# Two layers of graph and expert blocks: 12 instead of 8 of 16 node groups routed, in parts of 5 and 7, with the first part's pairs beside the second part's lists

## The chip, the cores and the metric

The kernel runs on one core of one Trainium2 chip. The time is device microseconds of one execution, given as the median of several runs. Its engines are PE (matrix multiply), DVE (vector), ACT (activation), POOL (which here mostly issues indirect DMAs) and SP (which issues the plain DMAs). They run side by side and meet at semaphores. "PEld" is the loading of weights into PE.

## The reference

The input is x, 128 graphs of 64 nodes with 256 features (8192 nodes), and an adjacency array. Two layers follow, each a graph block and an expert block, with residuals. The change concerns the last block alone, the expert block of layer 1:

```python
h = (x_flat @ W_gat).reshape(M, HEADS, NUM_EXPERTS)            # 4 heads, 4 experts
e = leaky_relu(a_src[src] + a_dst[dst])                         # 1,048,576 edges and loops
alpha = exp(e - e_max[dst]) / denom[dst]
agg = segment_sum(h[src] * alpha[:, :, None], dst)              # per node
scores = _layernorm(agg, ln_gamma, ln_beta).reshape(M, HEADS, NUM_EXPERTS).mean(1)
topk_s, topk_i = top_k(scores, 2)
w = softmax(topk_s)
for ei in range(NUM_EXPERTS):
    g = where(topk_i == ei, w, 0).sum(-1)
    hh = gelu(x @ W1[ei] + b1[ei])                              # 256 -> 512
    out = out + g[..., None] * (hh @ W2[ei] + b2[ei])           # 512 -> 256
```

Each node needs two of four experts, but which two is known only when the sums over its edges are there.

## The kernel before

The 8192 nodes are 64 tiles of 128, in 16 groups (`NG`) of four tiles (`GR`). All of x stays in SBUF. Layer 0 takes about the first 1000 us and is not touched. Layer 1 has these stages, with the times of the profiled execution:

**Graph stage** (1000 to 1381 us). A loop over steps `s` moves the groups through five streams (`back`, `first`, `second`, `combine`, `tables`), each some steps behind the other. `tables(g)` writes the normalised group to HBM: transposed to `zts` for a dense group, plain to `zns` for a routed one. It also writes the node table `tsrc` that the edges read.

**Dense groups.** A group of the first `DENSE` = 8 is put through all four experts without waiting for the gates. The generator `units` (lines 1129 to 1148) yields after every piece of that work: an expert has eight units, four of "h" (256 to 512, line 1101, with a gelu on ACT) and four of "y" (512 to 256, line 1111, with a bias add on DVE, line 1115). There are 256 units. As long as the gates aren't known, the y's are stored in `ystore` (128 KB each) and added later by `kept()`; once `adds` is filled, they are added at once, times the gate. Units need only the weights and `zts`, so they can stand beside anything. The graph stage takes 56 of them: from step 12 on, `quota` says how many follow each round of the streams.

**Prologue** (1381 to 1425 us): 20 units beside the set-up of the edge work.

**Lists** (1425 to 1706 us). The edges were sorted earlier into 16 lists, one for each group of destination nodes; `lists` has those of the routed groups first. `edges_of_lists` has 9 steps (`ET`) a list, 162 in all with the tail of its pipeline. Every step has an indirect gather of 128 rows of `tsrc` by POOL (line 1578, tile `got`) and a small copy, and by its place in the list the steps also sort a later list (lines 1507 to 1556), find the destinations' values (`to`, `pd`, `one`, `fd`), make the messages and one-hot matrices (`ol`, `r`) and sum them by matmul (line 1623) into `acc`. Three of four steps are followed by a unit. Every third step clears 256 KB of `zslots`.

**Gates, route, send.** When a part's lists are in `acc`, `gates` (27 yields, nearly all DVE) makes its two weights a node, and `route` (8 yields) finds for each node the two rows that it gets in the experts' slots (`place`) and which expert each slot belongs to (`pair_e`). `send` loads each tile of `zns` back, copies it twice into `y` tiles and scatters them to `zslots[h]` with two indirect DMAs by POOL (line 1897). The 8 routed groups are two parts of four groups, 16 tiles, 32 sends each. The first part's sends end beside units, at 1742 us; while they go, the dense groups' gates are made.

**Pairs** (1742 to 2028 us). A pair is two tiles of slots of one expert. A part has `PAIRS` = 19 (16 and three for experts that end within a pair). `load` (line 2014) reads the pair's expert into registers, then SP issues `zin` (256 KB), `w1e` (512 KB), `b1e` and `b2e`, two pairs ahead; `turned` transposes `zin`; h and y follow (lines 2059 and 2072), and y goes to `yslots[h]`. A pair has seven yields. Beside the first part's pairs stand the second part's sends, one at every third yield; beside the second part's pairs stands `back(0)`.

**Return and tail** (2028 to 2101 us). `back(h)` gathers a tile's two results from `yslots[h]` by POOL (line 2093), copies them, and adds them with their weights (line 2104) to x, which is then stored. `back(1)` needs all of the second part's y's, and stands beside the last 40 units.

The order on each engine comes from the framework: program order gives priorities, and it may issue an instruction earlier where its inputs and buffers are there. `paced_copy` and `tc.issue_after` put an instruction behind a given one on its engine. A pool's `bufs` says how many buffers each tile name has.

## Time and profile before

| | |
|---|---|
| median of 17 runs | 2104.31 us (2098.69 to 2109.7) |
| the profiled execution's own time | 2102.73 us |
| its span | 2101.0 us |
| busy: PE / PEld / DVE / ACT / POOL | 91% / 65% / 64% / 45% / 23% |
| PE: dense units, lines 1101 and 1111 | 512 and 1024 matmul records |
| PE: pairs, lines 2059 and 2072 | 139.2 and 137.8 us, 608 records each |
| POOL: gathers of line 1578 | 144, mean 1067 ns |
| POOL: sends of line 1897, returns of line 2093 | 64 each, mean 978 and 1002 ns |

The profile gives busy times by engine and by group of instructions, waits with what ended them, the chain of work that ended last, and sums over stretches of time. Busy PE time has modelled ends, and a matmul in 32 bit shows as two records. An engine's idle time costs something only where the chain passes through it.

### The profile page before, as it was taken

The page shows a single profiled execution, that of the slowest core. Times are in us where ns is not written, and L with a number is a line of the kernel's source. Part 1 is how long each engine was busy: PE and PEld are TensorE (multiplying, and loading weights), DVE is VectorE, ACT ScalarE, POOL GpSimd, SP SyncE. Part 2 cuts the span into 40 slices and gives each one's busy share as a digit, 9 for nine tenths or more (in the row PEclk, how much of TensorE's full clock was granted, in tenths as well). Part 3 has the DMA queues.
Part 4 walks back from the last instruction along what each step waited for, and adds up shares of the span by engine and source line. Part 5 has one row for each costly group of instructions (what it writes and reads, how often), then busy time and mean ns, then how long its engine had stood idle before and what let it go on. Part 6 is the DMA issues. An engine that isn't in the chain of part 4 may idle for free. (4 is left out here: it accounts for less than half of the span.)

```text
span 2101.0 us, 32601 instructions
## 1 busy us (share of the span) xinstructions
PE 1915.8 (91%) x10566; PEld 1371.3 (65%) x10566; DVE 1338.3 (64%) x4351; ACT 939.4 (45%) x1719; POOL 493.6 (23%) x528
## 2 busy tenths in 40 slices
PE   7889989899976999999578899998999999999999
PEld 5444545454435899898346667766667767888876
DVE  6889888842115888886697755756688451333435
ACT  4867766767641222221365565432333333333432
POOL 2013122132230000000530100004566552303223
PEclk9999999999997999999787899999999999999999
DMA  8022223233227555544214101282223248978943
GB/s 241 27 93 103 90 86 110 80 132 126 102 102 222 163 159 152 161 153 133 83 52 147 52 32 62 97 236 70 53 64 64 49 152 250 296 256 271 285 128 98
DMA packets 229376, 274.96 MB, mean 131 GB/s; under 512 B 57936, under 2 KB 173520, under 8 KB 229200
## 3 DMA queue, kind: packets, MB, share of 16 engines
q1 hardware_dynamic: 194288, 212.26, 32.6%
q0 software_dynamic: 24064, 60.22, 9.1%
q8 instruction: 89, 1.46, 0.3%
q10 hardware_dynamic: 10848, 0.30, 0.3%
q14 instruction: 87, 0.71, 0.1%
HBM read 159.40 MB, written 113.22 MB: 130 GB/s over the span
## 5 line engine op out<-in xcount | busy, mean ns | idle before, releaser
L464 PE MATMUL ph<-zT,w 128*128 128x512 f32 x512 | 249.0, 611 | 5.2 <-ACT zT L700 3.8
L969 PE MATMUL py<-wd,hTt 128*128 x1088 | 247.2, 381 | 0.0
L969 PEld LDWEIGHTS py<-wd,hTt 128*128 128x128 f32 x1088 | 202.5, 191 | 25.0
L954 ACT COPY hTt<-th 128x512 f32<-128x512 f32 x136 | 73.2, 589 | 299.7 <-PE th L951 299.7
L773 POOL DMA_INDIRECT hrows<-rows,pos x128 | 128.0, 1000 | 306.7 <-issue 189.0
L1578 POOL DMA_INDIRECT got<-tsrc,esrc x144 | 153.6, 1067 | 193.6 <-DMA ystore<-y 84.5
L1111 PE MATMUL py<-w,hT 128*128 128x256 f32 x800 | 190.5, 389 | 8.1 <-DVE td L1939 4.2
L1101 PE MATMUL ph<-zT,w 128*128 128x512 f32 x400 | 183.2, 599 | 0.0
L1180 POOL DMA_INDIRECT yin<-yrows,row_y x64 | 63.1, 987 | 485.8 <-SPq L1024 370.1
L1111 PEld LDWEIGHTS py<-w,hT 128*128 128x128 f32 x800 | 150.4, 193 | 38.6 <-issue 10.8
L464 PEld LDWEIGHTS ph<-zT,w 128*128 128x128 f32 x512 | 94.0, 195 | 106.5 <-issue 87.8
L1105 ACT ACTIVATE hT<-ph,b 128x512 f32<-128x512 f32 x100 | 68.6, 688 | 196.1 <-PE ph L1101 173.5
L2063 ACT ACTIVATE hT<-ph,b1e 128x256 f32<-128x256 f32 x152 | 72.1, 474 | 177.1 <-PE ph L2059 104.0
L2059 PE MATMUL ph<-zTp,w1e 128*128 128x256 f32 x608 | 139.2, 382 | 3.7 <-DMA w1e<-in_L_ffn_W_dram 3.7
L2072 PE MATMUL py<-w,hT 128*128 x608 | 137.8, 379 | 0.9 <-issue 0.9
L2080 DVE TENSOR_TENSOR y<-py,b2e 128x256 f32<-128x256 f32 x76 | 32.3, 425 | 156.0 <-PE py L2072 144.5
L2059 PEld LDWEIGHTS ph<-zTp,w1e 128*128 128x128 f32 x608 | 116.6, 192 | 20.2 <-issue 4.0
L626 PE MATMUL pre<-wd 128*128 128x512 f32 x256 | 124.2, 602 | 1.9 <-ACT wd L612 1.3
L467 ACT ACTIVATE hT<-ph,b 128x512 f32<-128x512 f32 x128 | 88.0, 687 | 77.3 <-PE ph L464 59.6
L2072 PEld LDWEIGHTS py<-w,hT 128*128 128x128 f32 x608 | 112.6, 190 | 15.1 <-issue 1.3
L1101 PEld LDWEIGHTS ph<-zT,w 128*128 128x128 f32 x400 | 73.0, 190 | 70.9 <-issue 69.8
L201 DVE TENSOR_TENSOR one<-iota_l,pb 128x2048 bf16<-128x2048 bf16 x96 | 116.8, 1217 | 0.2
(413 smaller groups left out, 3737.0 us busy)
## 6 DMA issues: line engine op xcount, KB each, us to landing
hin<-hrows SPq DMA_DIRECT2D x136, 256.0 KB
w1e<-in_L_ffn_W_dram SPq DMA_DIRECT2D x38, 512.0 KB
yin<-ystore SPq DMA_DIRECT2D x24, 512.0 KB
ystore<-y SPq DMA_DIRECT2D x80, 128.0 KB
zslots<-none SPq DMA_DIRECT2D x38, 256.0 KB
zin<-zslots SPq DMA_DIRECT2D x38, 256.0 KB
yslots<-y SPq DMA_DIRECT2D x76, 128.0 KB
bd<-in_L_ffn_bd_dram SPq DMA_DIRECT2D x68, 128.0 KB
```

What stands on the lines that cost most here:

```text
L201: V.tensor_tensor(o, numbers.unsqueeze(1).to_broadcast(shape), of.rearrange("p (j e) -> p j e", e=2).unsqueeze(2).to_broadcast(shape), ALU ...
L464: nc.tensor.matmul(ph, w1[:, c, q * P : q * P + P], zT[:, c, :], start=(c == 0), stop=(c == 1))
L467: gelus.append(S.activation(hT, ph, AF.Gelu, bias=b1[:, q : q + 1]).ins)
L626: nc.tensor.matmul(pre, xnT[:, c, n * P : n * P + P], wcat[:, c, :], start=(c == 0), stop=(c == 1),)
L773: nc.gpsimd.indirect_dma_start(to, bass.IndirectOffsetOnAxis(ap=pos[:, t : t + 1], axis=0), of[:, k, :], None)
L954: S.copy(hT[:, i : i + GR, :].rearrange("p q n -> p (q n)"), th)
L969: nc.tensor.matmul(py, hT[:, q, :], wd[:, bass.ds(e, 1), q, :].rearrange("p e f -> p (e f)"), start=(q == 0), stop=(q == NH - 1),)
L1101: nc.tensor.matmul(ph, w1[:, e, c, q * P : q * P + P], zT[:, c, :], start=(c == 0), stop=(c == 1))
L1111: nc.tensor.matmul(py, hTs[q][:, k * P : k * P + P], w2[:, e, q, :], start=(q == 0), stop=(q == NH1 - 1))
L1578: nc.gpsimd.indirect_dma_start(got, None, tsrc, bass.IndirectOffsetOnAxis(ap=esrc[:, b, at : at + 1], axis=0))
L2059: nc.tensor.matmul(ph, w1e[:, c, q * P : q * P + P], zT[:, c, :], start=(c == 0), stop=(c == 1))
L2072: nc.tensor.matmul(py, hTs[q][:, k * P : k * P + P], w2[:, e, q, :].rearrange("p e f -> p (e f)"), start=(q == 0), stop=(q == NH1 - 1),)
```

## The change

The first 5 and then 7 groups after the dense ones are routed, so that 4 groups are dense (128 units) and 12 routed (20 and 28 tiles; 23 and 31 pairs; 40 and 56 sends and as many returns). In the graph stage one unit follows the third round of each step from step 12 on. The pools of the lists, gates, sends and pairs are all open together; to that end most of the lists' tiles become single, the pools of hT and y tiles get 6 and 4 buffers instead of 8 and 6, `zin` two and `zTp` one instead of three, `kept` loads one expert's 128 KB at a time, `back` gathers into the space of `ts` and `td` and adds from there without a copy, and `td3` lies in that of `on`. `gates` works in place in `acc`.

The order is written anew: 55 list steps with a unit at every other; the first part's routing, three yields to each step and unit; its sends, two to a unit; eight more units behind the first loads of the pairs. Then come the pairs. Beside the first part's stand five list steps to six yields, up to the end of the second part's lists, then its routing, two yields at a time, then its sends, one at a yield. Beside the second part's pairs stand the remaining steps (those of the dense groups' lists), the dense groups' gates, then `kept`, and `back(0)` at every third yield. The last 24 units stand beside `back(1)`, two yields to a unit. A slot pair is cleared at every step until all 54 are.

```diff
-PARTS = 2
-ROUTED = 4 * PARTS
-DENSE = NG - ROUTED
-RT = ROUTED // PARTS * GR
-PAIRS = RT + 3
+ROUTED = (5, 7)
+PARTS = len(ROUTED)
+DENSE = NG - sum(ROUTED)
+RT = [GR * n for n in ROUTED]
+T0 = [GR * (DENSE + sum(ROUTED[:h])) for h in range(PARTS)]
+PAIRS = [n + NEXP - 1 for n in RT]
...
-                at = s - TABLES - 2
-                if s >= NG + SECOND:
-                    quota = int(r < 3)
-                elif at >= 0:
-                    quota = (2 * (at % 2), 2 * (at % 2), 4 - 4 * (at % 2), 0, 0, 0, 0, 0)[r]
-                else:
-                    quota = 0
+                quota = int(s >= TABLES + 2 and r == 2)
...
-    def edges_of_lists(pool, psum, td3):
+    def edges_of_lists(pool, one_each, psum, td3):
...
-                    el = pool.tile([P, ET * P], BF16, name="el")
+                    el = one_each.tile([P, ET * P], BF16, name="el")
...
-    hp = ctx.enter_context(tc.tile_pool(name="hp", bufs=8, reuse_waits="tile"))
-    yp = ctx.enter_context(tc.tile_pool(name="yp", bufs=6, reuse_waits="tile"))
+    hp = ctx.enter_context(tc.tile_pool(name="hp", bufs=6, reuse_waits="tile"))
+    yp = ctx.enter_context(tc.tile_pool(name="yp", bufs=4, reuse_waits="tile"))
...
             for j in range(2):
                 z = to["y"]()
                 paced_copy(z, zn)
-                sent = nc.gpsimd.indirect_dma_start(
+                row = nc.gpsimd.indirect_dma_start(
                     zslots[h], bass.IndirectOffsetOnAxis(ap=place[h][:, j, t : t + 1], axis=0), z, None
                 )
                 for other in sends:
-                    tc.declare_no_dep(sent.ins, other, reason="no two write the same row")
-                sends.append(sent.ins)
+                    tc.declare_no_dep(row.ins, other, reason="no two write the same row")
+                sends.append(row.ins)
                 yield
...
-        steps = routes()
-        zeros = ((h, i) for h in range(PARTS) for i in range(PAIRS))
-        for taken, _ in enumerate(edges_of_lists(emp, psm, td3)):
-
-            if taken % 3 == 0:
-                for h, i in zeros:
-                    nc.sync.dma_start(
-                        zslots[h][2 * P * i : 2 * P * i + 2 * P].rearrange("(k p) f -> p k f", p=P),
-                        none.unsqueeze(1).to_broadcast([P, 2, D]),
...
-            if taken > ET * (ROUTED // PARTS + 2):
-                next(steps, None)
-
-            if taken >= ET * NB:
-                next(sending)
-            if taken % 4 != 3:
-                next(units)
-        for _ in steps:
-            pass
+        sent.append(h)
...
+    KEEP = 1
...
-        ts = [t for t in range(T0) if n_kept[t // GR]]
-        for n in range(len(ts) + 1):
-            if n < len(ts):
-                g, k = divmod(ts[n], GR)
-                ys[n] = f2.tile([P, NEXP * D], F32, name="yin")[:, 0 : n_kept[g] * D]
+        of = [
+            (t, e, min(KEEP, n_kept[t // GR] - e))
+            for t in range(T0[0])
+            for e in range(0, n_kept[t // GR], KEEP)
+        ]
+        for n in range(len(of) + 1):
+            if n < len(of):
+                t, e, m = of[n]
+                g, k = divmod(t, GR)
+                ys[n] = f2.tile([P, KEEP * D], F32, name="yin")[:, 0 : m * D]
                 with tc.issue_after(behind[0]):
-                    nc.sync.dma_start(ys[n], ystore[g, k, :, 0 : n_kept[g] * D])
+                    nc.sync.dma_start(ys[n], ystore[g, k, :, e * D : (e + m) * D])
...
-    with tc.tile_pool(name="gd", bufs=1, reuse_waits="tile") as gd:
-        steps = gates(gd, 0, T0, {})
-        for _ in sending:
-            next(steps, None)
-            next(steps, None)
-            g, n = next(units)
-        for _ in steps:
-            pass
-        while (n + 1) % (NH1 + GR):
-            g, n = next(units)
-    adds.append(add)
...
-            z = fp.tile([P, 2, D], F32, name="zin")
+            z = fz.tile([P, 2, D], F32, name="zin")
...
-            zT = fp.tile([P, 2, 2 * P], F32, name="zTp")
+            zT = fo.tile([P, 2, 2 * P], F32, name="zTp")
         loaded = [load(*of[0]), load(*of[1])]
+        yield
...
+    backs = [ts.rearrange("p t c -> p (t c)")[:, D * i : D * i + D] for i in range(5)]
+    backs += [td.rearrange("p t c -> p (t c)")[:, D * i : D * i + D] for i in range(2)]
+
         later = 5
-        got, ys = {}, {}
-        for n in range(2 * RT + later):
-            if n < 2 * RT:
+        got = {}
+        for n in range(2 * RT[h] + later):
+            if n < 2 * RT[h]:
                 t, j = divmod(n, 2)
-                got[n] = fa.tile([P, D], F32, name="back")
+                got[n] = backs[n % len(backs)]
                 nc.gpsimd.indirect_dma_start(
                     got[n], None, yslots[h], bass.IndirectOffsetOnAxis(ap=place[h][:, j, t : t + 1], axis=0)
                 )
             if n >= later:
                 t, j = divmod(n - later, 2)
-                ys[j] = fb.tile([P, D], F32, name=f"yb{j}")
-                paced_copy(ys[j], got.pop(n - later))
+                at = T0[h] + t
+                xs = x[:, at, :]
+                with tc.issue_after(sums[0]):
+                    V.scalar_tensor_tensor(
+                        xs, got.pop(n - later), weight[h][:, j, t : t + 1], xs, ALU.mult, ALU.add
+                    )
                 if j:
-                    at = T0 + h * RT + t
-                    xs = x[:, at, :]
-                    for j in range(2):
-                        V.scalar_tensor_tensor(xs, ys[j], weight[h][:, j, t : t + 1], xs, ALU.mult, ALU.add)
                     behind[:] = [nc.sync.dma_start(out_t[:, at, :], xs).ins]
             yield
 
-    stored = kept()
-    with tc.tile_pool(name="fp", bufs=3, reuse_waits="tile") as fp:
-
-
-        moves = {0: send(1, sz), 1: back(0)}
-        for n, h in enumerate(pairs()):
-            if n % 3 == 2:
-                next(moves[h], None)
-            if n % 9 == 8:
-                next(stored, None)
-    for _ in moves[1]:
-        pass
-    steps = back(PARTS - 1)
-    for n, _ in enumerate(units):
-        next(steps, None)
-        if n % 3 == 2:
+    def enter(name, bufs, **more):
+        return ctx.enter_context(tc.tile_pool(name=name, bufs=bufs, reuse_waits="tile", **more))
+
+    sz, ga, em, em1, f2 = enter("sz", 2), enter("ga", 1), enter("em", 2), enter("em1", 1), enter("f2", 2)
+    fp, fz, fo, psm = enter("fp", 3), enter("fz", 2), enter("fo", 1), enter("psm", 1, space=PSUM)
...
+    n_td = NT * 2 * HEADS
+    td3 = on.rearrange("p t j -> p (t j)").bitcast(BF16)[:, 0 : 3 * n_td].rearrange("p (j c) -> p j c", j=3)
+    left_over = td.rearrange("p t c -> p (t c)")
...
+    zeros = ((h, i) for h in range(PARTS) for i in range(PAIRS[h]))
+    the_lists = edges_of_lists(em, em1, psm, td3)
+    taken = 0
+
+    def step():
+
+        nonlocal taken
+        for h, i in islice(zeros, 1):
+            nc.sync.dma_start(
+                zslots[h][2 * P * i : 2 * P * i + 2 * P].rearrange("(k p) f -> p k f", p=P),
+                none.unsqueeze(1).to_broadcast([P, 2, D]),
+            )
+        taken += 1
+        next(the_lists, None)
+
+    def unit():
+
+        nonlocal g, n
+        g, n = next(units)
+
+    def part(h):
+
+        ranks = {}
+        yield from gates(ga, T0[h], T0[h] + RT[h], ranks)
+        yield from route(h, ga, ranks, to["ph"])
+
+    def ends(h):
+        return ET * sum(ROUTED[: h + 1]) + ET + 1
+
+    def advance(it, n):
+        for _ in range(n):
+            next(it, None)
+
...
+    while taken < ends(0):
+        step()
+        if taken % 2:
+            unit()
+    routing = part(0)
+    while next(routing, 0) is None:
+        advance(routing, 2)
+        step()
+        unit()
+    sending = send(0, sz)
+    for i, _ in enumerate(sending):
+        if i % 2:
+            unit()
+    while (n + 1) % (NH1 + GR):
+        unit()
+    the_pairs = pairs()
+    next(the_pairs)
+    for _ in range(NH1 + GR):
+        unit()
+
+    def beside_first():
+
+        for i in range(ET * 100):
+            if taken >= ends(1):
+                break
+            if i % 6 != 5:
+                step()
+            yield
+        routing = part(1)
+        while next(routing, 0) is None:
+            next(routing, None)
+            yield
+        yield from send(1, sz)
+
+    def beside_second():
+
+        while taken < ET * (NB + 2):
+            step()
+            yield
+        yield from gates(ga, 0, T0[0], {})
+
+    adds.append(add)
+    beside = [beside_first(), beside_second()]
+    returned, stored = back(0), kept()
+    for i, h in enumerate(the_pairs):
+        if next(beside[h], 0) == 0 and h and i % 5 == 4:
             next(stored, None)
-    for of in (stored, steps):
+        if h and i % 3 == 2:
+            next(returned, None)
+    for of in (*beside, returned):
+        for _ in of:
+            pass
+    returned = back(1)
+    for _ in units:
+        advance(returned, 2)
+        next(stored, None)
+    for of in (stored, returned):
         for _ in of:
             pass
```

## The prediction

> **What bounds the kernel now.** I read the busy table first: PE 91%, DVE 64%, POOL 23%, so PE leads, but as a mean over stages. The chain of waits then shows the end of the run as one unbroken row of PE work, with one hole:
>
> ```profile
> 1735.26 5.19 PE py L1111 x24
> 1742.01 4.21 DMA w1e<-in_L_ffn_W_dram
> 1746.35 5.38 PE ph L2059 x16
> ...
> 2006.58 3.45 PE ph L2059 x16
> 2010.47 3.46 PE py L2072 x16
> 2013.92 3.45 PE ph L2059 x16
> ...
> 2083.27 6.87 PE ph L1101 x16
> 2090.13 6.92 PE py L1111 x32
> ```
>
> Columns: start, length, what. They give the two prices of everything below. A dense expert is 6.87 + 6.92 = 13.79 us, eight units of 1.72. A pair is 2013.92 - 2006.58 = 7.34 us, seven yields of 1.05. The hole is the first pair waiting: SP issues zin, which waits for the sends, and w1e is queued behind it on SP.
>
> The sums over stretches say which stage is limited by what (columns: length, busy and count of PE, PEld, DVE, ACT, POOL, then clock, DMA share, GB/s):
>
> ```profile
> 1240.00:1300.00 60.00, 55.87 (x241) 40.48 (x241) 37.72 (x119) 36.56 (x67) 0.00 (x0) 0.87 0.11 38
> 1425.00:1706.00 281.00, 274.91 (x1814) 192.59 (x1814) 195.94 (x726) 98.47 (x194) 163.82 (x154) 0.99 0.28 68
> 1706.00:1742.00 36.00, 32.93 (x113) 22.53 (x113) 14.41 (x53) 9.14 (x17) 17.02 (x18) 0.95 0.43 145
> 1800.00:1850.00 50.00, 50.00 (x247) 44.05 (x246) 15.63 (x38) 20.23 (x47) 15.31 (x16) 1.00 0.89 287
> 2028.00:2101.00 73.00, 69.04 (x241) 45.41 (x239) 34.65 (x89) 18.43 (x36) 31.49 (x32) 1.00 0.34 104
> ```
>
> The first row is the graph stage, where PE is nearly full at a reduced clock. Then: lists beside dense units (PE 275 of 281 us), rest of the sends, pairs (PE full, DMA 0.89), tail (five experts beside 32 returns). From 1425 on, PE sets the time, and about 14 us of 676 are idle. The third price is POOL's, from its timeline in the tail:
>
> ```profile
> 2032.71 0.95 POOL L2093 DMA_INDIRECT back<-yslots,place  x1 [0.30 <-ACT hT L1105]
> 2033.97 0.95 POOL L2093 DMA_INDIRECT back<-yslots,place  x1 [0.31 <-issue]
> ```
>
> With nothing in its way, one indirect transfer occupies POOL for 1.25 us. The fourth is the lists' PE work, from the groups:
>
> ```profile
> L1623 PE MATMUL ps<-r,ol 128*128 128x80 f32 x288 | 34.9, 273 | 1.7 <-DVE r L1495 1.7
> L1528 PE MATMUL ps<-kt,rows 128*128 128x27 bf16 x384 | 16.4, 175 | 4.1 <-DVE acc L1628 2.2 <-DVE rows L201 1.9
> L1591 PE MATMUL pd<-td,to 128*128 128x32 bf16 x432 | 13.6, 177 | 0.0
> ```
>
> That is 64.9 us over 16 lists; with transposes and edges, 4.3 us a list. It checks: 122 units x 1.72 + 16 x 4.3 = 279 of the 281 us.
>
> **The change, by stage.** PE loses 16 experts (220.6 us) and gains 16 pairs (117.4): 103 us less. The question is how much survives. Dense units fall from 256 to 128, and they were what filled PE while other engines prepared. Counted from the loops, they go: graph stage 16 (56 before), prologue 20 (20), lists of part 0 28, its routing 12, its sends 20, then 8, and 24 in the tail (40).
>
> *Graph stage.* 40 units leave, 68.8 us of PE if PE were the only limit. Adds of line 1295 two steps apart start 47, 46 and 45 us apart with eight units in them, 34 us (1120.8 to 1154.6) with almost none. With two units I take 36.5, so three periods give 28.5, the next two 11.5, and the last steps from 1354 to 1381, nearly all units, 12. Gain about 50 (38 to 65).
>
> The clock matters here. In the trace the granted clock is 0.51 from 1187 to 1201, although PE's longest shown wait between 1180 and 1300 is 2.4 us. [...]
>
> *Lists of part 0: 55 steps, 28 units.* PE: 28 x 1.72 + 5 x 4.3 = 70 us. POOL: 49 gathers (five were fetched ahead before) x 1.25 to 1.37 = 61 to 67. DVE: its list work summed over the stage is 155 us plus 12.5 of copies, 10.5 a list, so 52 + 14 adds x 0.42 = 58. Three engines at 60 to 70 us stall one another; zslots is now cleared at every step instead of every third, 54 writes of 256 KB; el, already waited for in four lists (8.8 us together), loads beside that. I add 8 for these and 3 for a PE that loses its full clock as in the row just shown: 81 us (73 to 92). The single tiles cost nothing by themselves: each is read in program order before its next writer, and PE follows that order closely. If DVE had to wait for PE it would be about 1 us a list, inside this range.
>
> *Routing of part 0: 12 steps, 12 units.* PE 26 us, but the end is set by DVE's chain: gates for 32 tiles with a nearly free DVE took 24 us (1693.8 to 1717.8), route of one part 8 us (1634.3 to 1642.3). For 20 tiles about 27, with 12 steps (14 us) and six adds between: 42 us (32 to 50).
>
> *Sends of part 0: 40 on POOL, 20 + 8 units (48 us of PE).* Before, the unhindered sends came 1.27 to 1.46 us apart; 40 x 1.31 = 52, and from the last send to the first pair's matmul it was 1734.84 to 1746.35, 11.5: 64 us (60 to 75). In these two stages PE idles some 30 us; before, they were hidden in the lists. Queued behind each send on POOL are the next gathers; nobody else waits for POOL here.
>
> *Pairs.* 54 x 7.34 = 396.4; the 9.7 remaining lists' PE work 42: 438. Beside part 0 come 51 steps in 61 yields: PE 88, POOL 51 x 1.3 = 66, DVE 67; hidden, and 7 us for small stalls. Then part 1 is routed and sent before its first pair: 33 us of DVE chain (28 tiles), 56 sends, 11.5 to the first matmul. PE has 100 yields, 105 us, to cover this. At POOL's 1.31 the chain is 118 us. But the packets of a send beside the pairs ended 3.6 to 4.8 us after its start, against 2.0 unloaded; yp has four buffers instead of six and the pairs' own y's share them, about 1.55 us a send: 131 us. At 1.9 it is 151; with the chain fully covered, 0. I take 28 lost (0 to 46). Demand then is a pair's 1.15 MB per 7.34 us plus 192 KB a send, near the 287 GB/s of the table. zT single, zin double and hp six cost nothing: their writers come after PE's last read in program order. In part 1, 26 gathers and 9 returns are 46 us on POOL against 40 of PE: in the 7. Pairs: 438 + 7 + 28 = 473.
>
> *Tail.* 24 experts' units are 41 us of PE, but 56 returns hang on the last pair's store: first one 3.4 us after the pairs' end as before, 55 x 1.31 = 72, landing and add 2.6, store 3: 81 us (77 to 88) against 73. Adding straight from the gathered tile saves a copy of 0.3 to 0.4 us on ACT or DVE, which set nothing here. The kept sums in quarters, the moved td3 and the masks: 0, unless yin comes late in the tail, where DVE has 50 of 81 us to do.
>
> *Sum* from 1425.3: -50 + 81 + 42 + 64 + 473 + 81 = 2116.3 against a span of 2101.0: +15.3. The profiled execution took 2102.73, 1.6 below the median of 17, 2104.31; so 2119.6.
>
> **Rivals.**
> 1. *Forecast: slower.* PE's 103 us go into the uncovered routing and sends (30 + 28), the POOL-bound tail (+8, with 41 of PE in it that shorten nothing) and a graph stage that gives 50 of 69. 2120; chance 0.44, its own range 2108.5 to 2140.
> 2. *Faster: the queues are filled across the stages.* The framework orders each engine's queue itself; part 0's gates ran at 1506.9, ahead of their place in the loop. If it issues list steps into the two holes, the pairs shorten by as much. Against it: at 1742 PE stood idle 4 us with 40 units left. Price up to 58; from 20 us filled on the kernel is faster. Half filled with a graph gain of 60: 2120 - 29 - 10 = 2081. Chance 0.36.
> 3. *Slower by more: sends under load.* At 1.9 us a send, lists at 92 and routing at 50: 2120 + 18 + 11 + 8 = 2157. Chance 0.10.
> 4. *No difference*, within 2100.1 to 2108.5: partial filling. Chance 0.10.
>
> That the change does not do what it says would be a graph stage no shorter, its DVE setting the time: 2120 + 50. The 34 us period speaks against; it is inside 3.
>
> **How the numbers follow.** A median of this kernel can be told from no change at about 0.2%, 4.2 us. Faster 0.36, same 0.10, slower 0.54. The range takes most of 2 and half of 3: 2070 to 2152.
>
> **What would show it.** Right: graph stage ends near 1331, first pair's matmul near 1562, pairs end near 2035, POOL gapless in the tail at 1.3 us, PE idle 25 to 35 us before the first pairs and again before part 1. Wrong: PE above 95% from the lists to the tail; or a tail shorter than 73 us; or the sends beside pairs at 1.3 us and no wait for zin.

## The result, and where the time went

The kernel after takes 2209.52 us (median of 8 runs, 2203.43 to 2215.81) against 2104.3 for the kernel before: ratio 1.0496, 95% interval 1.048 to 1.0512. The forecast was 2120 with a range up to 2152. The sign was right, and the loss is 105 us instead of 15.

The sessions fell into two conditions, told apart by the kernel before, which takes 2080 to 2083 us in one and 2103 to 2104 in the other, so every ratio is against the kernel before of the same session. In the first condition the unchanged kernel after (run c0_after) takes 2144.63 us where before takes 2081.91: ratio 1.0302 (1.0275 to 1.033). The same program thus loses 63 us in one condition and 105 in the other. (The expectations call the conditions chips, but chip 8 was met in both, with g6_order in the first and e8b_all in the second.)

The page of the kernel after, busy times:

```profile
PE 1887.6 (85%) x10374; PEld 1368.4 (62%) x10374; DVE 1309.3 (59%) x4258; ACT 924.3 (42%) x1728; POOL 552.9 (25%) x597
```

PE fell from 1915.8 us (91%) to 1887.6 (85%), so work did go. But 2213.2 less 1887.6 leaves 326 us without a matmul, and 2101.0 less 1915.8 left 185. Its chain of waits (start, length, what) no longer is one row of PE:

```profile
1603.15 5.15 DMA zslots<-y,place
1608.32 2.65 DMA zin<-zslots
1611.67 1.08 PE ps L1622 x10
1612.75 3.50 PE ph L1999 x16
...
1746.66 2.07 issue
1750.23 4.65 DMA zslots<-y,place
1754.88 2.06 issue
1757.54 1.98 issue
1762.70 4.25 DMA zn<-zns
...
1821.93 3.52 PE py L2012 x14
1825.46 3.45 PE ph L1999 x16
```

The first hole is the one forecast: last send, zin, first pair at 1612.75. The second, from 1729 to 1822, was not expected in this place: pairs of part 0 are under way, and the chain runs through sends. The sums over stretches of the kernel after (length, busy and count of PE, PEld, DVE, ACT, POOL, then clock, DMA share, GB/s):

```profile
1320.00:1352.00 32.00, 23.38 (x101) 19.92 (x101) 19.05 (x97) 5.35 (x9) 0.24 (x1) 0.53 0.47 153
1352.00:1411.00 59.00, 43.01 (x190) 25.58 (x191) 27.18 (x82) 11.79 (x16) 7.62 (x19) 0.85 0.79 222
1411.00:1507.00 96.00, 77.28 (x543) 55.47 (x543) 56.82 (x203) 23.59 (x50) 53.85 (x51) 0.87 0.28 70
1544.00:1612.00 68.00, 53.83 (x169) 34.08 (x168) 12.78 (x38) 14.17 (x29) 38.11 (x40) 0.90 0.53 172
1729.00:1824.00 95.00, 72.40 (x302) 57.41 (x300) 11.58 (x33) 31.63 (x81) 52.97 (x56) 0.89 0.67 210
1824.00:1924.00 100.00, 87.74 (x475) 72.88 (x474) 30.43 (x85) 32.26 (x73) 38.47 (x40) 0.85 0.48 136
1924.00:2116.00 192.00, 189.90 (x929) 167.00 (x928) 58.34 (x165) 65.26 (x132) 24.44 (x26) 1.00 0.68 201
2116.00:2213.00 97.00, 50.02 (x147) 31.08 (x146) 44.36 (x105) 7.81 (x12) 55.12 (x56) 0.75 0.54 159
```

Read the PE column against the length and then the clock. Of these rows only the pairs without lists (1924 to 2116) are still full. The end of the graph stage (1320) runs at a clock of 0.53, the prologue (1352) has PE for 43 of 59 us, and the tail (2116) for 50 of 97.

By the stages of the prediction, in us; the third column is the same kernel in the other condition. A stage ends where the timeline shows the last list's add, the first send, the first pair's matmul, the last pair's matmul:

| stage | predicted | after | c0_after |
|---|---|---|---|
| graph stage and prologue, against before | -50 | -14.5 | -18.1 |
| lists of part 0 | 81 | 96.6 | 75.6 |
| routing of part 0 | 42 | 36.2 | 36.2 |
| sends, to the first pair's matmul | 64 | 69.0 | 66.5 |
| pairs | 473 | 503.6 | 485.0 |
| tail | 81 | 97.0 | 85.7 |

(For c0_after "before" is the run e4_before_y4 below, whose lists start at 1416.1; in the trace of before they start at 1425.3.) The graph stage itself begins at other times from trace to trace, though the change leaves what lies in front of it as it was: its first table step comes between 1096 and 1105 us in the first condition and between 1110 and 1122 in the other. Counted from that step to the lists' start, the gain is 21 us in after (294.2 instead of 315.1) as well as in c0_after (293.2 instead of 314.5). From the lists' start on, the sum 741 nearly met the 749.0 of c0_after, partly because misses offset each other (lists 5 and routing 6 under, pairs 12 and tail 5 over); there the miss is the first row, 32 of 40 us. In the other condition the same stages take 802.4 us, 53 more than in c0_after, in lists, pairs and tail.

### The profile page after: what moved, and what is told of

The parts are those of the page before. It is cut to its first block, busy times and chain, and to the rows that moved or that the text cites. A ratio compares the mean times of both kernels' runs of the same rounds, so it can differ in the third digit from the quotient of the medians.

```text
span 2213.2 us, 32732 instructions
## 1 busy us (share of the span) xinstructions
PE 1887.6 (85%) x10374; PEld 1368.4 (62%) x10374; DVE 1309.3 (59%) x4258; ACT 924.3 (42%) x1728; POOL 552.9 (25%) x597
## 5 line engine op out<-in xcount | busy, mean ns | idle before, releaser
L466 PE MATMUL ph<-zT,w 128*128 128x512 f32 x512 | 248.6, 610 | 5.7 <-ACT zT L702 4.3
L2012 PE MATMUL py<-w,hT 128*128 x864 | 218.4, 402 | 29.5 <-ACT hT L2003 14.8
L2003 ACT ACTIVATE hT<-ph,b1e 128x256 f32<-128x256 f32 x216 | 100.6, 473 | 258.4 <-PE ph L1999 202.7
L1999 PE MATMUL ph<-zTp,w1e 128*128 128x256 f32 x864 | 203.9, 384 | 4.3 <-issue 4.2
L2020 DVE TENSOR_TENSOR y<-py,b2e 128x256 f32<-128x256 f32 x108 | 45.7, 423 | 239.1 <-PE py L2012 176.3
L1999 PEld LDWEIGHTS ph<-zTp,w1e 128*128 128x128 f32 x864 | 163.2, 192 | 27.4 <-issue 6.1
L1113 PE MATMUL py<-w,hT 128*128 128x256 f32 x448 | 127.5, 437 | 53.1 <-ACT hT L1107 22.8
L466 PEld LDWEIGHTS ph<-zT,w 128*128 128x128 f32 x512 | 93.5, 195 | 107.3 <-issue 88.1
L469 ACT ACTIVATE hT<-ph,b 128x512 f32<-128x512 f32 x128 | 87.8, 686 | 77.0 <-PE ph L466 60.7
L2036 POOL DMA_INDIRECT ts<-yslots,place x70 | 68.5, 979 | 198.3 <-DMA yin<-ystore 110.9
L1107 ACT ACTIVATE hT<-ph,b 128x512 f32<-128x512 f32 x56 | 37.9, 687 | 189.1 <-PE ph L1103 108.8
L1905 POOL DMA_INDIRECT zslots<-y,place x96 | 92.2, 961 | 93.5 <-ACT y L1129 42.7
```

Source lines behind the costliest of these rows:

```text
L466: nc.tensor.matmul(ph, w1[:, c, q * P : q * P + P], zT[:, c, :], start=(c == 0), stop=(c == 1))
L1113: nc.tensor.matmul(py, hTs[q][:, k * P : k * P + P], w2[:, e, q, :], start=(q == 0), stop=(q == NH1 - 1))
L1905: row = nc.gpsimd.indirect_dma_start(zslots[h], bass.IndirectOffsetOnAxis(ap=place[h][:, j, t : t + 1], axis=0), z, None)
L1999: nc.tensor.matmul(ph, w1e[:, c, q * P : q * P + P], zT[:, c, :], start=(c == 0), stop=(c == 1))
L2003: pace[:] = [S, S.activation(hT, ph, AF.Gelu, bias=b1e[:, q : q + 1]).ins]
L2012: nc.tensor.matmul(py, hTs[q][:, k * P : k * P + P], w2[:, e, q, :].rearrange("p e f -> p (e f)"), start=(q == 0), stop=(q == NH1 - 1),)
```

## The experiments

**One part undone at a time.** Ratios are against before; the kernel after is 1.0302 in this condition (before 2083.04 for the first four, 2081.91 for the others).

*More y buffers* (e1_y8):

```diff
-    hp = ... name="hp", bufs=6      yp = ... name="yp", bufs=4
+    hp = ... name="hp", bufs=4      yp = ... name="yp", bufs=8
```

> The kernel after with eight y buffers instead of four, paid for with four hidden-layer buffers instead of six (there is no other room). Theory 'y buffers': in the sends of part 1 PE had 66 of 88 us because each send holds a y buffer until it has landed and the pairs' own y's take the same four; with eight the waits of DVE and ACT for a send's landing (61 us added up from 1733 to 1821) go, the 56 sends come at about 1.35 us instead of 1.71, part 0's 40 at 1.3 instead of 1.52, and the run is 20 to 35 us shorter, 2175 to 2190. Rival 'POOL and the transfers themselves': the sends keep 1.6 to 1.7 us and the run moves by 5 us or less. If the hidden-layer buffers matter, the dense units' period grows and the run is longer.

Measured: 2111.72, ratio 1.0148 (1.0121 to 1.0175), 1.5% or 32 us less. The sends of part 1, first in c0_after, then with eight buffers (same columns as above):

```profile
1688.00:1785.00 97.00, 74.46 (x300) 58.92 (x299) 11.45 (x32) 31.23 (x82) 52.82 (x55) 0.84 0.66 205
```

```profile
1667.00:1742.00 75.00, 66.61 (x301) 53.81 (x300) 11.38 (x33) 31.11 (x81) 52.87 (x56) 0.98 0.83 265
```

The same 300 matmuls and the same 56 sends fit in 75 instead of 97 us. POOL is busy for the same 53 us, so it was not the limit, and DMA goes from 205 to 265 GB/s, so neither were the transfers. The waits tell what was; engine and line, waited for, total, times, longest, c0_after first:

```profile
DVE y L2020 <- DMA zslots<-y,place: 39.6, 7, 8.8
ACT y L1129 <- DMA zslots<-y,place: 21.2, 10, 4.3
```

```profile
DVE y L2020 <- DMA zslots<-y,place: 14.5, 3, 7.1
```

The pairs' own y adds (L2020) stood 39.6 us for a send to land, and PE behind them. The wait of ACT's copies (L1129) for a send fell from 21.2 to 3.3 us; with eight buffers these copies wait 28.6 us for the loads of `zn` instead. Part 0's sends fell from 56.5 to 49.4 us. (The graph stage also began 8 us earlier in this trace, unexplained.) And of the 22 us in the rows, 8 are PE's own: 74.46 busy at a clock of 0.84 against 66.61 at 0.98. Eight is more than the six of the kernel before, so what the step from six to four cost was not measured by itself.

*td's split behind the prologue* (e2_td3):

```diff
+    with tc.issue_after(sums[0]):
         for j in range(3):
             V.tensor_copy(td3[:, j, :], left_over)
...
```

> The kernel after, with the split of td into three bf16 terms issued behind the last add of the prologue. Theory: the split, free to start early since it now lies in the tile of the on-table, was pulled into the prologue, where DVE stood 10.9 us behind the DMA that loads td; that is why the prologue took 59.0 us instead of 41.5. Put behind, the prologue takes 42 to 46 us and the run is 8 to 17 us shorter (2193 to 2201). Rival: the stall only takes the place of another wait (the first list's gathers), the lists start at the same time, and the run moves by 3 us or less.

The stall, in the kernel after's timeline of DVE:

```profile
1356.83 0.42 DVE L1438 TENSOR_TENSOR up<-up,td 128x256 f32<-128x256 f32 x1
1368.11 0.69 DVE L2084 TENSOR_TENSOR td<-td,on 128x512 f32<-128x512 f32 x1 [10.86 <-DMA tdst<-td]
```

DVE stands 10.86 us for a store that reads td, with the prologue's y adds queued behind it, and PE behind those. Measured: 2134.88, ratio 1.0243 (1.0223 to 1.0264), 12 us less; prologue 46.0 instead of 56.7 us. As the theory said.

*The graph stage's units in its last steps* (e3_late):

```diff
-                quota = int(s >= TABLES + 2 and r == 2)
+                quota = int(s >= NG + SECOND and r < 3)
```

> The kernel after, with the graph stage's 16 dense units all in its last steps, three a step as those steps had them before, instead of one a step throughout. Theory 'clock': in the last five steps of the graph stage PE had too little to keep its full clock (0.53 from 1320 to 1352) and lost what the removed units gave; with units there the clock is above 0.9, the first prologue expert starts 5 to 12 us earlier and the run is about 10 us shorter (2197 to 2205). Rival: the last steps are set by DVE's and ACT's chain; the units then only move, and the run is within 4 us of 2209.5.

Measured: 2126.1, ratio 1.0212 (1.0183 to 1.024), 19 us less. The last steps in c0_after, then here:

```profile
1315.00:1341.00 26.00, 18.01 (x77) 15.38 (x77) 16.11 (x80) 4.28 (x7) 0.24 (x1) 0.50 0.51 163
```

```profile
1303.00:1325.00 22.00, 19.38 (x117) 15.72 (x117) 16.38 (x83) 4.96 (x8) 0.24 (x1) 0.97 0.55 182
```

117 matmuls at a clock of 0.97 take less time than 77 at 0.50: dense units put there cost less than nothing. From the first table step to the first expert of the prologue it is 15.2 us less (221.3 instead of 236.5): 10 of them in the steps before, which now have no units, and 5 in the last steps, which now have all of them.

*Kept sums before the tail* (e6_kept): `i % 5 == 4` becomes `i % 2`.

> The kernel after, with the kept sums advanced at every second yield of part 1's pairs instead of every fifth, so that nearly all of them are loaded and added before the last pair. Theory 'kept sums in the tail': the 56 returns of the tail come at 1.48 us because DVE's returns wait behind adds whose yin is late (13.9 us of such waits) and POOL waits for DVE (14.1 us); then the tail falls from 97 us towards 81 and the run is 8 to 16 us shorter (2193 to 2201). Rival: the returns are set by POOL and the landing of the gathers themselves, the tail keeps 92 to 97 us, and the run is the same or, with more transfers beside the pairs, a few us longer.

Measured: 2164.58, ratio 1.0369 (1.033 to 1.0407), 14 us more. The tail moved by 2 us (83.2), the rival's side, and part 1's pairs after the lists took 215 instead of 192 us: DVE stood behind the loads there, and PE behind DVE.

```profile
DVE x L1915 <- DMA yin<-ystore: 91.8, 38, 7.3
```

*Part 0's returns behind part 1's lists* (e5_back_late): `next(returned)` moves into the branch taken once `beside` is exhausted.

> The kernel after, with the returns of part 0 and the kept sums only advanced once part 1's remaining lists and gates are done. Theory: in the first 115 us of part 1's pairs PE was busy for 100 because returns and gathers share POOL's queue (returns wait for the pairs' adds, and the gathers behind them); with the returns behind the lists this stretch is 5 to 12 us shorter, and the run too. Rival: the lists' own chain on DVE sets that stretch; the run moves by 3 us or less, or the returns reach into the tail and it is up to 10 us longer.

Measured: 2133.48, ratio 1.0247 (1.0217 to 1.0277), 11 us less. From part 1's first pair to the last list it is 53.2 instead of 59.8 us, the rest of the 11 lies in other stages.

*The buffers alone, in the old order* (e4_before_y4): the kernel before with 6 hT and 4 y buffers.

> The kernel before with the y buffers of the kernel after (four instead of six) and its six hidden-layer buffers instead of eight: this part of the change alone, in the old order of stages. Theory 'y buffers': its 96 sends run beside dense units and pairs as well, so it gets 15 to 35 us slower. Rival 'order': in the old order the sends are three units or yields apart and a buffer is always free in time, so it moves by less than 4 us, and the buffers only cost because the change sends one after another.

Measured: 2084.25, ratio 1.0015 (1.0002 to 1.0028): 3 us, 6 at most. The rival held: the 32 us of e1_y8 (there from four to eight buffers) come only with the new order, where sends follow one another with nothing between them.

**Three edits together** (e7_comb), e1, e2 and e3:

> The kernel after with the three edits that gave stages back: eight y buffers with four hidden-layer buffers, td's split behind the prologue's last add, and the graph stage's 16 units in its last steps. If the three gains lie in different stages and add up (sends of part 0 49 instead of 58 us, of part 1 75 instead of 96, prologue 46 instead of 56, last graph steps 18 instead of 23), the run takes 2068 to 2090 us where the kernel before takes 2083. If they overlap, 2095 to 2110.

Measured: 2090.54, ratio 1.0042 (1.0025 to 1.0059). Of the 63 us lost, 54 are back; the three alone add up to 63. The lists start at 1368.0, 48 us ahead of the old order's 1416.1 (3 of them because the graph stage began earlier): the -50 of the forecast is nearly there as soon as td's split and the place of the 16 units are mended.

> The kernel after once more, unchanged, for a time on the same chip as the experiments. The kernel before took 2083.0 us beside the first four experiments and 2104.3 beside the kernel after. From the stages of the first four (graph start 1107, to the first pair 469, pairs 486, tail 85) the kernel after should take 2147 us where before takes 2083, a ratio of 1.031. Rival: the ratio of 1.050 holds everywhere (2187 us beside 2083); then the first four changes are each worth 50 us more than their stages show.

(That was the control; 1.0302, as the first four runs' stages said.)

**The order with the same matmuls** (g6_order): `ROUTED = (4, 4)` and the graph stage's units as before.

> The kernel after with parts of 4 and 4 groups and the graph stage's dense units as the kernel before had them: the same matmuls as before, in the new order of stages (a part's lists, routing and sends ahead of its pairs, the rest beside pairs), with the new buffers. Theory 'the order costs, the routed groups gain': the prologue's stall (16 us), part 0's routing and sends bare of dense work (25 us) and the y buffers (15 to 25) make it 45 to 75 us slower than before on a chip where before takes 2082 (ratio 1.022 to 1.036), and 60 to 100 where before takes 2104; its tail is full of dense units and shows no late PE completions. Rival 'the routed groups cost': with the same matmuls as before the order costs less than 15 us, and most of the 62 (or 105) us come with the four groups more.

Measured: 2171.64 beside 2079.55, ratio 1.043 (1.0395 to 1.0465), 92 us more. The theory named the right side and was too small (45 to 75). The order with its new buffers costs more than the whole change, and routing four groups more gives back about 27 (1.030 against 1.043). From the lists' start to the end, e4_before_y4 first (three rows), then three of the new order's rows:

```profile
1416.00:1730.00 314.00, 307.07 (x1931) 215.68 (x1932) 211.16 (x779) 108.33 (x212) 181.46 (x171) 0.99 0.31 81
1730.00:2011.00 281.00, 281.00 (x1365) 247.08 (x1365) 99.13 (x233) 103.92 (x235) 63.52 (x64) 0.99 0.82 261
2011.00:2084.00 73.00, 69.03 (x241) 45.41 (x239) 34.70 (x89) 18.41 (x36) 31.74 (x32) 0.99 0.34 104
```

```profile
1512.00:1574.00 62.00, 49.34 (x156) 30.24 (x155) 13.52 (x44) 13.94 (x29) 31.89 (x32) 0.89 0.56 178
1634.00:1692.00 58.00, 45.75 (x187) 36.79 (x186) 7.90 (x24) 18.94 (x48) 30.08 (x32) 0.88 0.65 206
1745.00:1873.00 128.00, 110.79 (x827) 93.92 (x827) 69.25 (x214) 52.03 (x122) 90.71 (x87) 0.93 0.55 148
```

The first three add up to 668 us with PE busy for 657. In the new order the same stretch (1423 to 2165) is 742 us with 682 busy: 49 us more idle, and 25 us more for the same matmuls; 50 us of PE's work fell into stretches of half clock, 12 in e4_before_y4. The three rows are the holes: sends of part 0, sends of part 1, and the last lists beside pairs.

**The other condition** (before 2103). *All four edits* (e8_all: e7 and e5; e8b_all the same again):

> The kernel after with all four edits that gained alone: eight y buffers (four hidden-layer ones), td's split behind the prologue, the graph stage's units in its last steps, and part 0's returns and the kept sums behind part 1's lists. Before beside it about 2082. If the last edit's 11 us add to the other three (2090.5 with them), 2077 to 2083, no different from before. Rival: the stretch it shortened is now set by the lists' own chain on DVE; 2086 to 2092.

> The kernel with all four edits (parts of 5 and 7) once more, for its time on another chip. It took 2171 where before takes 2103. Without part 0's returns put back it took 2090.5 where before takes 2082. If the last edit's 11 us add there: ratio 0.997 to 1.001 where before takes about 2080; where before takes 2104 again 1.03.

Measured: 2171.05, ratio 1.0306 (1.0265 to 1.0346), and 2170.64, 1.0326 (1.0306 to 1.0345). Both fell in this condition, so the 2077 to 2083 of the other were not seen. The edits give back 36 to 40 of 105 us here; part 0's lists still take 90.7 to 97.6 us, and the tail 95.

*The lists' tiles single, in the old order* (e11_single, e11b_single):

```diff
-                    el = pool.tile([P, ET * P], BF16, name="el")
+                    el = one_each.tile([P, ET * P], BF16, name="el")
...
```

> The kernel before with the lists' tiles single (those that the kernel after made single: el, to, oh, one, fd, msg, z, ol and the spread message), in the old order of stages. The prediction put this part of the change at 0. If so, within 4 us of before (2078 to 2086). Rival: el can only be loaded once the list before has read it, and its landing, 12 to 15 us after its issue in the trace of after, then sets the period of a list (about 15 us) or DVE waits for PE to have read the one-hot tiles: PE's lists stage of 281 us gets 5 to 25 us longer.

> The kernel before with the lists' tiles single, once more on another chip. It was 13 us slower (ratio 1.005) on the chip where before takes 2103. If the cost belongs to the single tiles, it is 8 to 15 us slower on every chip; if to that chip's late PE completions, which DVE must wait for when a tile has no second buffer, then 0 to 4 us where before takes about 2080.

Measured: 2116.49, ratio 1.005 (1.0025 to 1.0074), and 2114.58, 1.0048 (1.0028 to 1.0069): 11 to 13 us, not 0. In the second trace the lists' start to the first pair is 326.9 instead of 321.1 us, so some 6 us lie where the tiles are, and 5 in front of the graph stage, where the edit changes nothing. Whether they cost anything in the faster condition was not seen. The landing 12 to 15 us after el's issue, by which e11_single's rival goes, is not in the trace of after: the packets of six of its loads from 1435 on end 2.7 to 3.4 us after the issue.

*Parts of 6 and 6*, alone (e9a_66) and with the four edits (e9_66):

> The kernel after with parts of 6 and 6 instead of 5 and 7, nothing else. After took 2144.6 beside a before of 2082. Theory as for the other one with 6 and 6: tail 10 us shorter, sends of part 1 eight fewer at 1.7 us, part 0 about 5 us longer: 2120 to 2136. Rival (the split does not matter while y buffers and clock set the pace): 2139 to 2150.

> As the one with all four edits, but with parts of 6 and 6 groups instead of 5 and 7. Theory: what remains lost sits where the second part is larger than the first: 56 returns in the tail at 1.27 us beside only 41 us of PE work, and 56 sends and the routing behind 23 pairs. With 6 and 6 the tail has 48 returns (75 instead of 85 us), 27 pairs cover 48 sends, and part 0 pays one list and 8 sends more, most of it beside units taken from the tail: 15 to 25 us less than with 5 and 7, 2055 to 2067, faster than the kernel before (2082). Rival: part 0's longer lists and sends lie bare before the first pair and eat the gain: within 6 us of 5 and 7.

Measured: ratios 1.056 (1.0522 to 1.0599) and 1.0434 (1.0395 to 1.0473), both slower than 5 and 7. The bare part grew as said (first pair 18 to 20 us later), and the expected gain in the tail went to the kept sums: with fewer units to stand beside, the last one was added 26 and 28 us after the last return instead of 8 us ahead of it (after). So the split itself is not settled.

*Fewer units beside part 0's lists* (e13_fewer): `taken % 2` becomes `taken % 3 == 1`, and one or two returns a unit.

> As the one with all four edits, but part 0's lists take a dense unit at every third step instead of every second (18 instead of 28), so that 10 units (17 us of PE) go to the tail, where PE works 47 of 85 us; the tail's returns are spread over its 34 units. Theory: part 0's lists were full of PE work (72 of 75 us) and come down to POOL's and DVE's 62 to 66, while the tail hides the units: 6 to 11 us faster than all four edits, 2067 to 2074 where before takes 2080, faster than both kernels. Rival: the lists are set by the chain from gather to add, not by PE: the lists keep 72 to 75 us, the tail gets the units' 5 to 10 us on top, and it is slower.

Measured: 2180.66, ratio 1.0374 (1.0356 to 1.0391), 10 us slower than e8b_all: the rival. That run's lists first, then e13's:

```profile
1383.00:1473.00 90.00, 78.00 (x541) 54.53 (x542) 57.88 (x203) 22.23 (x49) 53.71 (x49) 0.88 0.31 80
```

```profile
1380.00:1476.00 96.00, 73.05 (x511) 50.53 (x511) 54.36 (x197) 22.60 (x48) 61.04 (x55) 0.82 0.27 69
```

Thirty matmul records less, no shorter, and a lower clock. In this condition PE did not set this stage, and taking work from it did not shorten it.

**Less routed, units as before** (before 2079.55), with the four edits: parts of 5 and 5 (h1_55), of 6 and 4 (h2_64).

> Parts of 5 and 5 groups, the four edits, and the graph stage's units as the kernel before had them. PE's work is 51 us less than before's (eight experts at 13.8 us against eight pairs at 7.34), and dense units are left for the tail (48, 83 us, against 40 returns of 1.27 us plus 14). Theory: about 30 us of holes remain before the first pairs and between the parts, so 10 to 25 us faster than before on a chip where before takes 2082 (ratio 0.988 to 0.995); on the chip where before takes 2104 it is 10 to 40 us slower than before, since the single tiles and the late PE completions of that chip show in the list stages. Rival: the order's holes stay as large as in the kernel after, and it is slower than before on both kinds of chip by 20 us or more.

> As the one with 5 and 5 groups, but 6 and 4: the part that runs bare is the larger, the tail's returns are 32 instead of 40. Theory: one more list (14 us, 11 of it PE work) and 8 more sends (10 us, 7 of it PE work) in front of the first pair; the sends of part 1 (32) are wholly covered by 27 pairs, so 8 to 12 us of the hole between the parts go. Within 8 us of 5 and 5. Rival: the bare stages weigh more: 10 to 20 us slower than 5 and 5.

Measured: 2126.37, ratio 1.0213 (1.018 to 1.0247), and 2170.92, 1.0429 (1.0393 to 1.0464). The first fell on its rival's side, the second 45 us behind the first, beyond its rival's 20, both by mechanisms that neither expectation names. With 5 and 5 there are 72 kept sums; 73 us pass after the last return (10 in the kernel after), DVE waiting 32.2 us for 24 loads of them, one a unit. With 6 and 4 part 0's returns, put back by the fourth edit, were not done when the pairs ended: the tail's first return comes 40 us after the last pair.

No kernel run here beat the kernel before; of those with the new order the nearest is e7_comb with 1.0042.

## Why the prediction was right in sign and wrong in size

**"Forecast: slower", by bare routing, bare sends and a tail that hangs on POOL:** right, and shown by g6_order, which has the order and its buffers but no group more. Its price was far too low. Of the 97 us by which the sum for the profiled execution missed, 35.5 lie in the graph stage and prologue, 15.6 in the lists, 30.6 in the pairs and 16 in the tail; routing and sends nearly cancel.

**The step that failed: "Graph stage ... Gain about 50 (38 to 65)", with prologue "20 (20)" and "the moved td3 and masks: 0".** Measured 14.5 (18.1 in c0_after), in three parts. From its first table step to the prologue the graph stage gained 38 us (235.2 instead of 273.6), the prologue lost 17.5, and the stage began 6 us later, which is not explained. By the adds that the forecast goes by (line 1295, in after 1297), the three periods gained 21 instead of 28.5, the next two 9 instead of 11.5, and the last steps 7 instead of 12. The 36.5 us taken for a period with two units were 39.0 in the mean, and 36.2 with no unit at all (e3_late). With all 16 units in the last steps (e3_late) the three marks give 30, 13 and 10, although the last steps then hold more work: their clock was 0.50 in c0_after and 0.97 in e3_late. So the forecast had no term for where the remaining units stand. And td3 at 0 was wrong: `on` is free long before the old place of td3, so the framework moved the split up into the prologue, where DVE stood 10.86 us for the store of td; the prologue took 59.0 us instead of 41.5, and in e2_td3, with the split put behind, 10.7 of them are back. With both mended, e7_comb gains 45 us from the first table step on.

**"zT single ... hp six cost nothing", single tiles 0:** hp right (e4_before_y4). The single tiles cost up to 6 us in their stage in the one condition in which they were measured. zT single and zin double were not tried alone.

**Sends "about 1.55 us", "I take 28 lost (0 to 46)":** the mechanism was right, down to the four y buffers; the size was 1.72 us a send (94.6 over 55 steps), and the sum put the loss at the wrong place. The chain's end was not what PE waited for in front of part 1; PE lost its time during the sends, by the pairs' own y's waiting for the same buffers. Behind the last send PE is full again, in c0_after (part 0's last pairs, then the last lists beside part 1's):

```profile
1785.00:1809.00 24.00, 24.00 (x119) 21.14 (x118) 2.96 (x7) 7.49 (x16) 0.96 (x1) 1.00 0.68 198
1809.00:1869.00 60.00, 53.01 (x362) 45.79 (x361) 27.90 (x78) 25.23 (x58) 37.30 (x39) 0.94 0.53 150
```

In c0_after the pairs' 485 lies 12 above the 473. PE's idle time in them adds up to 35 us, just the 7 and 28 of the forecast; as it lies elsewhere, that is luck.

**"3 for a PE that loses its full clock":** added up over the clock records, PE works at half clock for 10 us after the lists' start in before, 62 in c0_after and 94 in after. This term was 3 in one stage and missing in all others. In g6_order it is 50 us, and 25 us more of PE time on the same matmuls.

**Tail 81 (77 to 88):** 85.7 in c0_after, 97 in after, outside. Its first returns start 1.25 us apart, as said:

```profile
2121.06 0.95 POOL L2036 DMA_INDIRECT ts<-yslots,place  x1 [0.30 <-DVE x L1915]
2122.31 0.95 POOL L2036 DMA_INDIRECT ts<-yslots,place  x1 [0.30 <-issue]
```

Over all 56 it is 1.51, two stops of 4 and 7 us among them in which POOL waits for DVE's adds; in c0_after it is 1.30.

**What stays open.** 53 of the 97 us by which the stage sum missed in after are not there in c0_after, the same program: the lists are 21 longer in after, the tail 11, the pairs 19, nearly all beside the last four lists (100 us from 1824 against 84 in the two rows above), the sends 2. The steps that failed there are the 81 for the lists, the 473 for the pairs and the 81 for the tail, each outside its range in after only; why stays open. In those stages the trace of after has waits that no shown event explains. ACT in the tail of after, then in that of c0_after (last column: idle before, what ended it):

```profile
2167.20 0.69 ACT L1107 ACTIVATE hT<-ph,b 128x512 f32<-128x512 f32 x1 [22.29 <-remote]
2177.03 0.69 ACT L1107 ACTIVATE hT<-ph,b 128x512 f32<-128x512 f32 x1 [9.14 <-issue]
```

```profile
2078.20 0.69 ACT L1107 ACTIVATE hT<-ph,b 128x512 f32<-128x512 f32 x1 [8.77 <-PE ph L1103]
2079.92 0.69 ACT L1107 ACTIVATE hT<-ph,b 128x512 f32<-128x512 f32 x1 [1.03 <-PE ph L1103]
```

The matmuls that ACT needs ended at 2167.3 by the record, and ACT went on 9.7 us later, with PE idle behind it. At seven places of that trace four or more of PE's semaphore updates come within 0.2 us, in one of them (2142.4) five for matmuls that by the record ended at 2131.5 to 2138.4; in the trace of before that is so at one place (1902.1, for ends from 1899.1 on). By these records PE's completions were late there. Two things weaken this: the ends of matmuls are modelled, and the traces of after and of before lack semaphore updates (of PE's 1989 and 1997 they hold 1841 and 1842; in all 23,945 are recorded in after, 32,633 in c0_after), so a wait whose end is not shown may only have lost its record. Why the completions were late was not found: g6_order, meant to tell it by a full tail, ran in the faster condition, and no run isolates it.

## What to carry to other kernels

The dense units that filled PE between its waits also went with a higher clock (0.97 with 117 matmul records in e3_late's last graph steps, 0.50 with 77 in c0_after's) and covered the sends on POOL (PE is busy for 307 of 314 us in e4_before_y4's lists and sends, for 49 of 62 in g6_order's sends of part 0), so moving such work away can cost more than its own duration says: price the stage that it leaves, at the clock that the stage will then have. When a tile moves into space that is free earlier, its writers can move earlier too, and what waits in order behind them pays: td's split held DVE for 10.86 us, and behind the prologue's last add it gave 12 us back. Buffers shared by a stream and by the work that is to cover it must be counted for both at once; four buffers cost 3 us (1.0015) with work between the sends, and in the new order eight instead of four gave 32 us back.

## What the runs showed of the hardware

- PE took 682 us (g6_order) for the matmuls that took 657 in the old order (e4_before_y4), with 49 us more of idle scattered in. In the kernel after's graph stage there are six stretches of half clock (10 to 34 us) between 1147 and 1356 us, and the longest wait of PE that starts in the 12 us ahead of each is 1.5 to 2.9 us. In c0_after PE's longest wait is 2.9 us between 1110 and 1260, where the clock is 0.81 (1109 to 1260), and 2.5 us between 1315 and 1341, where it is 0.50. What lowers the clock was not shown.
- Fewer matmuls can take longer: 77 records in 26 us at a clock of 0.50 (c0_after) against 117 in 22 us at 0.97 (e3_late).
- The same program took 2144.6 us in one session and 2209.5 in another (3.0%), where the kernel before differs by 1.1%; of these two, the schedule with scattered holes varies more.
